# Spread of y about each partition's first channel, and an expert's transposes inside the next one's products

## The chip, the cores and the metric

The kernel runs on one core of one Trainium2 chip. The metric is the device time of one execution in microseconds, the median of three runs. One profiled execution of the same program gives the trace from which every other number here is taken.

## What is computed

The input x holds 4 sequences of 1024 tokens with 1024 channels. It is normalised over the channels (layernorm), and two branches are added to it:

```
xn  = layernorm(x)
out = x + attn(xn) + moe(xn)

attn:  q = xn @ Wq;  v = xn @ Wv                  # 16 heads of 64 channels
       state[t] = lam * state[t-1] + v[t]         # lam = sigmoid(beta), one for each head
       y  = q * state
       y  = (y - mean(y)) * rsqrt(var(y) + 1e-5) * ln_g + ln_b    # over the 1024 channels
       attn = (y * silu(xn @ Wg)) @ Wo

moe:   each of the 4096 tokens picks its best 8 of 64 experts (softmax of xn @ router.T);
       an expert takes at most the first 128 tokens that picked it
       h = silu(xg @ w1.T) * (xg @ v1.T);  yr = (h @ w2.T) * weight;  added back at the token's row
```

All data is fp32.

## The kernel before

**Attention part.** The four sequences (batches b = 0 to 3) are worked one after the other in `batch_row`. Channels lie on the 128 partitions, so a sequence's y is eight tiles of 128 partitions x 1024 tokens; y(c) is tile c, and a channel mean is a sum over the eight tiles and then over partitions. The tiles y(m) and y(m + 4) are made together in round m = 0 to 3: `states(m)` (v and the scan), then `queries(m)` (q times state). Four more rounds, `gates(m)`, follow.

Each round's matrix product is done with seven smaller products in place of eight (sums and differences of 512x512 blocks). `steps` writes them out. The blocks of xn are B11, B21, B22, B12 and their sums T1 to T4 (`right_sums`; T1 lies in B12's place); the results collect in three PSUM tags, a, b and c, of two banks each. The order on TensorE is B11 (bank a), B21 (b), then the last product of the round before, T1 (c), T2 (a), B22 (c), T3 (a), and T4 (a) only inside the next round. Between them ScalarE copies a bank (L148) and VectorE adds and reads the banks (L160, L169, L172).

In the records a fp32 product of 128x512 appears twice; `x8` in a profile line is four products.

**The statistics of y.** Variance is found from sums about a shift. After the first round (m = 0), `find_shift` takes sum1 = y(0) + y(4), has two products with the constant matrix mean_w spread the sum of all partitions (`all_channels`, tag r, one bank), and ScalarE copies it as `shift`. `less_shift` then subtracts the shift from each tile (VectorE, L621), squares it on ScalarE (L626), and GpSimd adds up squares and values (L627 sum2, L628 sum1). `find_spread` runs inside the product of `gates(0)`: two products for the mean, two for the mean square, VectorE subtracts (L661), ScalarE takes the root and VectorE the reciprocal (L663). `gates` then takes the mean from each tile (L677), scales by g and the reciprocal root (L678), adds b and multiplies by the gate (L681), and GpSimd's queue stores it to DRAM as `gated`.

In batch 0 the sums of the weight blocks (`left_sums`, L51 to L54) are made on GpSimd too, and tokens are chosen for the experts on VectorE meanwhile (`take`, the MAX8 and MATCH_REPLACE8 lines).

**Expert part.** `Experts.run` goes over the 64 experts. `hidden` makes two products of eight steps each (h in bank a and in bank b, 384 columns), ScalarE takes silu of the first (act), VectorE multiplies by the second. `output` turns act with three transposes on TensorE (hpt, L900), VectorE copies them out (hT, L901), six products give the expert's rows (y, L906), VectorE scales them (ys, L909), and GpSimd's queue adds them to `out` by an indirect DMA (L917). `fetch` loads the weights by SP's queue into the tiles that x and y had before, and gathers the tokens by GpSimd's queue (xg, L852) into the pool of nine blocks (`quarter`) that xn's blocks had; `turned` brings xg into the layout that TensorE wants (xgT, VectorE, L870). The products y @ Wo are spread as `project` over the experts, about a quarter of a unit for each. Wo's four blocks are loaded by `load_wo`, which also makes their sums T1 to T4 on VectorE (`right_sums`, four operations of 128x2048: L61, L64, L66, L68).

**What sets the order.** A scheduler orders each engine's instructions from the program text, and hands out the blocks of a pool in the order in which they come free. `in_order` pins the text's order for the engines that it is given; in the experts that is VectorE for the first three:

```
            kept = [mybir.EngineType.DVE] if e < 3 else []
            with in_order(self.tc, kept):
                act = self.hidden(e, self.turn)
                ...
                if before is not None:
                    self.output(*before)
```

Of the kernel before, what the change touches and what calls it, by code (L numbers as in the profile page):

```python
# [8 lines left out]
F32 = mybir.dt.float32  # L9
I32 = mybir.dt.int32  # L10
AF = mybir.ActivationFunctionType
ALU = mybir.AluOpType
# [4 lines left out]
P = 128  # L17
B, S, D = 4, 1024, 1024
NTOK = B * S
KD = D // P  # L20
# [77 lines left out]
class Pools:  # L98
# [21 lines left out]
    def y(self, name):  # L120
        return self.three.tile([P, 3, S], F32, tag="y", name=name)
# [111 lines left out]
def attn_and_routing(  # L233
# [345 lines left out]
    def batch_row(b, left):  # L579
# [5 lines left out]
        def y(c, cols=slice(0, S)):  # L585
            return ys[place[c] // 3][:, place[c] % 3, cols]

        shift = mean = ys[2][:, 2, :]
        sum1 = one.tile([P, S], F32, tag="sum1", name=f"sum1_{b}")
        sum2 = one.tile([P, S], F32, tag="sum2", name=f"sum2_{b}")  # L590
        spread = []
# [6 lines left out]
            )  # L598
            return ps

        def states(m, left, late):
# [9 lines left out]
            left = product(  # L611
                nc, pools, weights(b, 0, m), quarters[b],
                lo[:, H0], lo[:, H1], hi[:, H1], then, left, f"v_{b}_{m}", late,
                begun.get(0) if b == 0 and m == 0 else None,
            )
            return lo, hi, left

        def queries(m, lo, hi, left):
            def less_shift():
                for i, c in enumerate((m, m + KH)):  # L620
                    nc.vector.tensor_tensor(y(c), y(c), shift, ALU.subtract)  # L621
                    if m == 0 and i == 0:
                        nc.scalar.activation(sum2, y(c), AF.Square)
                        continue
                    sq = line.tile([P, S], F32, tag="line", name=f"sq_{b}_{c}")
                    nc.scalar.activation(sq, y(c), AF.Square)  # L626
                    nc.gpsimd.tensor_tensor(sum2, sum2, sq, ALU.add)  # L627
                    nc.gpsimd.tensor_tensor(sum1, y(0) if m == 0 else sum1, y(c), ALU.add)  # L628

            def find_shift():  # L630
                for h, cols in enumerate((H0, H1)):
                    ps = all_channels(sum1, h, f"sh_{b}_{h}")
                    nc.scalar.activation(shift[:, cols], ps, AF.Copy, scale=float(NM))
                less_shift()

            def then(c21):
                nc.vector.tensor_tensor(y(m + KH, H0), c21, hi[:, H0], ALU.mult)
                nc.vector.tensor_tensor(y(m), y(m), lo, ALU.mult)
                nc.vector.tensor_tensor(y(m + KH, H1), y(m + KH, H1), hi[:, H1], ALU.mult)
                if m == 0:  # L640
                    nc.gpsimd.tensor_tensor(sum1, y(0), y(KH), ALU.add)
                else:
                    less_shift()
# [6 lines left out]
            return left, find_shift if m == 0 else None  # L650

        def find_spread():

            for h, cols in enumerate((H0, H1)):
                ps = all_channels(sum1, h, f"mean_{b}_{h}")
                nc.scalar.copy(mean[:, cols], ps)
            rstd = one.tile([P, S], F32, tag="sum1", name=f"rstd_{b}")
            nc.scalar.activation(rstd, mean, AF.Square)
            for h, cols in enumerate((H0, H1)):
                ps = all_channels(sum2, h, f"var_{b}_{h}")  # L660
                nc.vector.tensor_tensor(rstd[:, cols], ps, rstd[:, cols], ALU.subtract)  # L661
            nc.scalar.activation(rstd, rstd, AF.Sqrt, bias=eps)
            nc.vector.reciprocal(rstd, rstd)  # L663
            spread.append(rstd)

        def gates(m, left):
            lo = line.tile([P, S], F32, tag="line", name=f"glo_{b}_{m}")
            hi = line.tile([P, S], F32, tag="line", name=f"ghi_{b}_{m}")

            def then(c21):  # L670
                (rstd,) = spread
                nc.scalar.activation(hi[:, H0], c21, AF.Silu)
                nc.scalar.activation(lo, lo, AF.Silu)
                nc.scalar.activation(hi[:, H1], hi[:, H1], AF.Silu)
                for i, (c, gate) in enumerate(((m, lo), (m + KH, hi))):
                    yc = y(c)
                    nc.vector.tensor_tensor(yc, yc, mean, ALU.subtract)  # L677
# [19 lines left out]
        late = None  # L697
        taking = take(b)
        for m in range(NM):
            lo, hi, left = states(m, left, late)  # L700
            if m == 0:
                route(b, logits[b])
            if b == 0 and m == 0:
# [8 lines left out]
            left, late = queries(m, lo, hi, left)  # L712
            next(taking)
            if b + 1 < B:
                if m == 1:
# [106 lines left out]
class Experts:  # L822
# [52 lines left out]
            self.tc.keep_in_program_order(done)  # L875
        return xT

    def hidden(self, e, xT):
        nc, pools = self.nc, self.pools
        ph = []  # L880
        for n in range(2):
            ps = pools.bank("ab"[n], [P, F], f"h{n}_{e}")
            w = self.weights.pop((e, n))
            for k in range(KD):
                nc.tensor.matmul(  # L885
                    ps, lhsT=xT[:, k, :], rhs=w[:, k, :], start=(k == 0), stop=(k == KD - 1)
                )
            ph.append(ps)
        act = pools.one.tile([P, F], F32, tag="cur", name=f"act_{e}")
        nc.scalar.activation(act, ph[0], AF.Silu)  # L890
        nc.vector.tensor_tensor(act, act, ph[1], ALU.mult)
        return act

    def output(self, e, act):
        nc, pools = self.nc, self.pools
        w2, wt = self.weights.pop((e, 2)), self.tokens.pop(e)[1]
        hT = pools.line.tile([P, KF, P], F32, tag="line", name=f"hT_{e}")
        pt = pools.bank("t", [P, KF, P], f"hpt_{e}")
        for j in range(KF):
            nc.tensor.transpose(pt[:, j, :], act[:, j * P : (j + 1) * P], self.ident)  # L900
        nc.vector.tensor_copy(hT, pt)  # L901
        ys = pools.line.tile([P, D], F32, tag="line", name=f"ys_{e}")
        for h, cols in enumerate((H0, H1)):
            ps = pools.bank("cr"[h], [P, SH], f"y_{e}_{h}")
# [21 lines left out]
    def load_wo(self):  # L926
        for name, (i, o) in zip(("B11", "B21", "B22", "B12"), BLOCKS):
            self.wo_b[name] = self.pools.block(f"wo_{name}")
            load_block(self.nc, self.wo_b[name], self.wo, i, o * SH, SH)
        right_sums(self.nc.vector, self.wo_b, lambda n: self.pools.block(f"wo_{n}"))  # L930

    def load_gated(self, u):
        t = self.pools.left.tile([P, NSLOT, KH, P], F32, tag="w", name=f"gated_{u}")
# [23 lines left out]
        self.turn = self.turned(0)  # L957

    def run(self):
        units = B * NM  # L960
        gated = self.load_gated(0)
        self.fetch(1)
        self.load_wo()
# [4 lines left out]
        before, todo, u, many = None, None, 0, iter(())  # L968
        for e in range(E):

            kept = [mybir.EngineType.DVE] if e < 3 else []
            with in_order(self.tc, kept):
                act = self.hidden(e, self.turn)
                self.fetch(e + 2)
                self.load(e + 1, 2)
                if e + 1 < E:
                    self.turn = self.turned(e + 1)
                if before is not None:
                    self.output(*before)
                before = e, act  # L980
                if u < units and e == begins[u]:
                    todo = self.project(u, gated)
# [54 lines left out]
```

## Time and profile before

| what | value |
|---|---|
| median of three runs | 2662.32 us (2661.1 to 2663.75) |
| the profiled execution | 2664.6 us, its span 2662.8 us |
| attention part | 0 to about 1237 us |
| expert part | about 1237 to 2662.8 us |
| TensorE busy | 2633.1 us, 6933 records |
| VectorE, ScalarE, GpSimd busy | 1086.5, 317.4, 732.9 us |
| mean granted TensorE clock | 0.997 |

The span is the time from the first to the last of the program's instructions. An engine's row of the timeline gives the start of a group, its length, the tile that it writes and those that it reads, and in square brackets the idle time of the engine just before it with what ended that. The stretch of half clock shows in the page's slices only as a share; the timeline shows it as groups that take twice their usual time.

### The profile page before, as it was taken

The page shows a single profiled execution, that of the slowest core. Times are in us where ns is not written, and L with a number is a line of the kernel's source. Part 1 is how long each engine was busy: PE and PEld are TensorE (multiplying, and loading weights), DVE is VectorE, ACT ScalarE, POOL GpSimd, SP SyncE. Part 2 cuts the span into 40 slices and gives each one's busy share as a digit, 9 for nine tenths or more (in the row PEclk, how much of TensorE's full clock was granted, in tenths as well). Part 3 has the DMA queues.
Part 4 walks back from the last instruction along what each step waited for, and adds up shares of the span by engine and source line. Part 5 has one row for each costly group of instructions (what it writes and reads, how often), then busy time and mean ns, then how long its engine had stood idle before and what let it go on. Part 6 is the DMA issues. An engine that isn't in the chain of part 4 may idle for free.

```text
span 2662.8 us, 18539 instructions
## 1 busy us (share of the span) xinstructions
PE 2633.1 (99%) x6933; PEld 1267.7 (48%) x6933; DVE 1086.5 (41%) x1394; ACT 317.4 (12%) x476; POOL 732.9 (28%) x655
## 2 busy tenths in 40 slices
PE   9999999999999999999999999999999999999997
PEld 5444444444444444444555555555555555555554
DVE  7945686465944685273222212222122221222211
ACT  4213112131212111121000000000000000000000
POOL 1453312121121102132333233332333333333321
PEclk9999999999999999999999999999999999999999
DMA  5665534452335522336889888898888988889886
GB/s 187 244 193 192 183 114 139 178 177 91 139 118 185 200 85 83 146 119 235 299 288 298 288 275 284 284 303 283 275 285 282 305 282 275 283 285 304 273 268 179
DMA packets 122473, 592.95 MB, mean 223 GB/s; under 512 B 15872, under 2 KB 52736, under 8 KB 89360
## 3 DMA queue, kind: packets, MB, share of 16 engines
q1 hardware_dynamic: 81488, 448.03, 46.4%
q0 software_dynamic: 40464, 143.72, 20.0%
q8 instruction: 55, 0.90, 0.1%
q14 instruction: 34, 0.28, 0.0%
q10 hardware_dynamic: 432, 0.01, 0.0%
HBM read 483.67 MB, written 124.81 MB: 229 GB/s over the span
## 4 chain that ended last, share of the span: by engine, by line
PE 94%; DVE 4%; issue 1%; DMA 0%; ACT 0%; POOL 0%; POOLq 0%; DVEq 0%
PE h L885 25%; PE y L906 13%; PE pa_o L137 8%; PE pa_g L137 8%; PE pa_q L137 7%; PE pa_v L137 7%; PE pc_o L137 4%; PE pc_v L137 4%; PE pc_g L137 4%; PE pc_q L137 4%; PE pb_o L137 2%; PE pb_g L137 2%; PE pb_q L137 2%; PE pb_v L137 2%; PE lg L475 1%; PE hpt L900 1%
## 5 line engine op out<-in xcount | busy, mean ns | idle before, releaser
L885 PE MATMUL h<-w,xgT 128*128 128x384 f32 x2048 | 672.2, 486 | 0.7 <-issue 0.7
L885 PEld LDWEIGHTS h<-w,xgT 128*128 128x128 f32 x2048 | 388.9, 190 | 286.2 <-issue 33.7
L852 POOL DMA_INDIRECT xg<-rows,tables x256 | 252.4, 986 | 679.8 <-DVE xgT L870 615.8
L906 PE MATMUL y<-w,hT 128*128 128x512 f32 x768 | 343.5, 597 | 1.6 <-DVE hT L901 1.6
L901 DVE COPY hT<-hpt 128x384 f32<-128x384 f32 x64 | 35.6, 556 | 729.1 <-PE hpt L900 729.1
L137 PE MATMUL pa_g<-xT,w 128*128 128x512 f32 x512 | 233.9, 600 | 2.7 <-DVE ghi L172 2.7
L906 PEld LDWEIGHTS y<-w,hT 128*128 128x128 f32 x768 | 140.9, 190 | 192.6 <-issue 153.3
L137 PE MATMUL pa_q<-xT,w 128*128 128x512 f32 x480 | 216.6, 593 | 3.8 <-DVE y L172 3.8
L137 PE MATMUL pa_v<-xT,w 128*128 128x512 f32 x480 | 216.5, 592 | 0.0
L909 DVE TENSOR_SCALAR ys<-y,wt 128x512 f32<-128x512 f32 x128 | 96.1, 751 | 202.2 <-PE y L906 199.7
L137 PE MATMUL pa_o<-wo_T,gated 128*128 128x512 f32 x384 | 177.8, 592 | 0.0
L137 PEld LDWEIGHTS pa_g<-xT,w 128*128 128x128 f32 x512 | 97.9, 192 | 127.1 <-issue 123.2
L137 PEld LDWEIGHTS pa_q<-xT,w 128*128 128x128 f32 x480 | 90.5, 190 | 116.8 <-issue 109.8
L137 PEld LDWEIGHTS pa_v<-xT,w 128*128 128x128 f32 x480 | 91.1, 190 | 114.9 <-issue 111.9
L890 ACT ACTIVATE act<-h 128x384 f32<-128x384 f32 x64 | 31.4, 490 | 848.6 <-PE hpt L900 833.3
L686 POOL DMA_DIRECT2D gated<-y x64 | 48.5, 763 | 301.3 <-DVE y L681 289.8
L917 POOL DMA_INDIRECT out_dram<-ys,tables x63 | 102.4, 1626 | 104.8 <-DMA out_dram<-ohi 76.1
L137 PE MATMUL pc_o<-wo_B,gated 128*128 128x512 f32 x256 | 117.1, 592 | 0.0
L137 PE MATMUL pc_g<-xT,w 128*128 128x512 f32 x256 | 115.2, 592 | 1.5 <-ACT sc_g L148 1.5
L137 PE MATMUL pc_v<-xT,w 128*128 128x512 f32 x256 | 115.3, 593 | 0.0
L137 PE MATMUL pc_q<-xT,w 128*128 128x512 f32 x256 | 115.2, 592 | 0.0
L628 POOL TENSOR_TENSOR sum<-sum,y 128x1024 f32<-128x1024 f32 x24 | 56.5, 2355 | 209.2 <-DVE y L621 209.2
(209 smaller groups left out, 2466.5 us busy)
## 6 DMA issues: line engine op xcount, KB each, us to landing
w<-in_w_dram SPq DMA_DIRECT2D x128, 1536.0 KB, 7.5
w<-in_v_dram SPq DMA_DIRECT2D x64, 1536.0 KB, 7.4
w<-wsum SPq DMA_DIRECT2D x36, 1792.0 KB, 8.1
wsum<-w POOLq DMA_DIRECT2D x12, 1792.0 KB, 6.5
x<-in_x_dram SPq DMA_DIRECT2D x32, 512.0 KB, 8.8
rows<-x POOLq DMA_DIRECT2D x32, 512.0 KB, 7.3
gated<-y POOLq DMA_DIRECT2D x64, 256.0 KB, 5.4
gated<-gated SPq DMA_DIRECT2D x16, 1024.0 KB, 8.1
```

What stands on the lines that cost most here:

```text
L137: nc.tensor.matmul(ps, lhsT=lhs[:, slot, k, :], rhs=blocks[right][:, k, :], start=start and k == 0, stop=stop and k == KH - 1, skip_group_ ...
L475: nc.tensor.matmul(two[h * E : (h + 1) * E, :], lhsT=r_sb[:, k, :], rhs=blocks[f"B{k // KH + 1}{h + 1}"][:, k % KH, :], start=(k == KD - 1 ...
L628: nc.gpsimd.tensor_tensor(sum1, y(0) if m == 0 else sum1, y(c), ALU.add)
L686: nc.gpsimd.dma_start(out=gated[b, :, :, slot, m, :].rearrange("u p j -> p u j"), in_=yc[:, h * SH : (h + 1) * SH].rearrange("p (u j) -> p ...
L852: nc.gpsimd.indirect_dma_start(out=xg[:, r, :], out_offset=None, in_=self.rows.rearrange("n (q c) -> (n q) c", q=NQ), in_offset=bass.Indir ...
L885: nc.tensor.matmul(ps, lhsT=xT[:, k, :], rhs=w[:, k, :], start=(k == 0), stop=(k == KD - 1))
L890: nc.scalar.activation(act, ph[0], AF.Silu)
L900: nc.tensor.transpose(pt[:, j, :], act[:, j * P : (j + 1) * P], self.ident)
L901: nc.vector.tensor_copy(hT, pt)
L906: nc.tensor.matmul(ps, lhsT=hT[:, j, :], rhs=w2[:, j, cols], start=(j == 0), stop=(j == KF - 1))
L909: nc.vector.tensor_scalar(ys[:, cols], ps, wt, None, ALU.mult)
L917: self.nc.gpsimd.indirect_dma_start(out=to, out_offset=bass.IndirectOffsetOnAxis(ap=rows, axis=0), in_=ys, in_offset=None, compute_op=ALU.add,
```

## The change

There are two parts.

In the statistics, the shift is no longer a mean that TensorE must find. Each tile's difference from y(0), the first channel of each partition, goes to a tile of its own (`away`), which ScalarE squares; y itself is not touched. `find_spread` corrects for the reference: with d = y(0) - mean, the sum of squares about the mean is sum2 + 2 d (sum1 - 8 y(0) + 4 d), worked out on VectorE in four operations (`off`). The sums of the last round (m = 3) go on VectorE, the others stay on GpSimd. The root is taken from the second product's bank by ScalarE directly, half by half.

In the experts, `turned_hidden` transposes the act of the expert before between the first and the second eight products of `hidden`, `output` follows with the six products, and the order on TensorE is pinned too for the first three experts. The sums of Wo leave `load_wo` and stand behind the gate of expert 0. The turn of the next expert's tokens stands behind the gate from expert 1 on.

```diff
-        shift = mean = ys[2][:, 2, :]
+        mean = ys[2][:, 2, :]
...
         def queries(m, lo, hi, left):
-            def less_shift():
-                for i, c in enumerate((m, m + KH)):
-                    nc.vector.tensor_tensor(y(c), y(c), shift, ALU.subtract)
-                    if m == 0 and i == 0:
-                        nc.scalar.activation(sum2, y(c), AF.Square)
-                        continue
-                    sq = line.tile([P, S], F32, tag="line", name=f"sq_{b}_{c}")
-                    nc.scalar.activation(sq, y(c), AF.Square)
-                    nc.gpsimd.tensor_tensor(sum2, sum2, sq, ALU.add)
-                    nc.gpsimd.tensor_tensor(sum1, y(0) if m == 0 else sum1, y(c), ALU.add)
-
-            def find_shift():
-                for h, cols in enumerate((H0, H1)):
-                    ps = all_channels(sum1, h, f"sh_{b}_{h}")
-                    nc.scalar.activation(shift[:, cols], ps, AF.Copy, scale=float(NM))
-                less_shift()
+            def collect(c):
+
+                add = (nc.vector if m == NM - 1 else nc.gpsimd).tensor_tensor
+                add(sum1, y(0) if c == KH else sum1, y(c), ALU.add)
+                away = line.tile([P, S], F32, tag="line", name=f"away_{b}_{c}")
+                nc.vector.tensor_tensor(away, y(c), y(0), ALU.subtract)
+                nc.scalar.activation(sum2 if c == KH else away, away, AF.Square)
+                if c != KH:
+                    add(sum2, sum2, away, ALU.add)
...
         def find_spread():
+            off = line.tile([P, S], F32, tag="line", name=f"off_{b}")
+            nc.vector.scalar_tensor_tensor(off, y(0), -float(KD), sum1, ALU.mult, ALU.add)
             for h, cols in enumerate((H0, H1)):
                 ps = all_channels(sum1, h, f"mean_{b}_{h}")
                 nc.scalar.copy(mean[:, cols], ps)
+            nc.vector.tensor_tensor(y(0), y(0), mean, ALU.subtract)
+            nc.vector.scalar_tensor_tensor(off, y(0), 0.5 * KD, off, ALU.mult, ALU.add)
+            nc.vector.tensor_tensor(off, off, y(0), ALU.mult)
+            nc.vector.scalar_tensor_tensor(sum2, off, 2.0, sum2, ALU.mult, ALU.add)
             rstd = one.tile([P, S], F32, tag="sum1", name=f"rstd_{b}")
-            nc.scalar.activation(rstd, mean, AF.Square)
             for h, cols in enumerate((H0, H1)):
                 ps = all_channels(sum2, h, f"var_{b}_{h}")
-                nc.vector.tensor_tensor(rstd[:, cols], ps, rstd[:, cols], ALU.subtract)
-            nc.scalar.activation(rstd, rstd, AF.Sqrt, bias=eps)
+                nc.scalar.activation(rstd[:, cols], ps, AF.Sqrt, bias=eps)
             nc.vector.reciprocal(rstd, rstd)
...
-    def hidden(self, e, xT):
+    def hidden(self, e, xT, before):
...
             ph.append(ps)
+            if n == 0 and before is not None:
+                hT = self.turned_hidden(*before)
+        return ph, hT
...
-        right_sums(self.nc.vector, self.wo_b, lambda n: self.pools.block(f"wo_{n}"))
...
-            kept = [mybir.EngineType.DVE] if e < 3 else []
+            kept = [mybir.EngineType.DVE, mybir.EngineType.PE] if e < 3 else []
             with in_order(self.tc, kept):
-                act = self.hidden(e, self.turn)
+                ph, turned_before = self.hidden(e, self.turn, before)
                 self.fetch(e + 2)
                 self.load(e + 1, 2)
-                if e + 1 < E:
+                if e == 0:
                     self.turn = self.turned(e + 1)
+                act = self.gate(e, ph)
+                if 0 < e < E - 1:
+                    self.turn = self.turned(e + 1)
+                if e == 0:
+                    right_sums(nc.vector, self.wo_b, lambda n: self.pools.block(f"wo_{n}"))
                 if before is not None:
-                    self.output(*before)
+                    self.output(*turned_before)
...
-        self.output(*before)
+        self.output(*self.turned_hidden(*before))
```

`turned_hidden` holds the transposes and the copy hT that stood in `output` before; `gate` holds the silu and the product that stood in `hidden`.

More of the change, by code (lines that the diff above doesn't have):

```diff
@@ L599, in all_channels, with states @@
             return ps
-        def states(m, left, late):
+        def states(m, left):
             lo = line.tile([P, S], F32, tag="line", name=f"lo_{b}_{m}")
@@ L612, in states @@
                 nc, pools, weights(b, 0, m), quarters[b],
-                lo[:, H0], lo[:, H1], hi[:, H1], then, left, f"v_{b}_{m}", late,
+                lo[:, H0], lo[:, H1], hi[:, H1], then, left, f"v_{b}_{m}", None,
                 begun.get(0) if b == 0 and m == 0 else None,
@@ L639, in then @@
                 nc.vector.tensor_tensor(y(m + KH, H1), y(m + KH, H1), hi[:, H1], ALU.mult)
[L640 to L643, printed above, removed]
+                for c in (m, m + KH):
+                    if c > 0:
+                        collect(c)
             left = product(
@@ L649, in queries @@
             )
-            return left, find_shift if m == 0 else None
+            return left
         def find_spread():
+            off = line.tile([P, S], F32, tag="line", name=f"off_{b}")
+            nc.vector.scalar_tensor_tensor(off, y(0), -float(KD), sum1, ALU.mult, ALU.add)
             for h, cols in enumerate((H0, H1)):
@@ L676, in then @@
                     yc = y(c)
-                    nc.vector.tensor_tensor(yc, yc, mean, ALU.subtract)
+                    if c > 0:
+                        nc.vector.tensor_tensor(yc, yc, mean, ALU.subtract)
                     nc.vector.scalar_tensor_tensor(
@@ L695, in gates @@
             )
-        late = None
         taking = take(b)
         for m in range(NM):
-            lo, hi, left = states(m, left, late)
+            lo, hi, left = states(m, left)
             if m == 0:
@@ L711, in batch_row @@
             next(taking)
-            left, late = queries(m, lo, hi, left)
+            left = queries(m, lo, hi, left)
             next(taking)
@@ L876, in turned @@
         return xT
-    def hidden(self, e, xT):
-        nc, pools = self.nc, self.pools
-        ph = []
+    def hidden(self, e, xT, before):
+        pools = self.pools
+        ph, hT = [], None
         for n in range(2):
@@ L884, in hidden @@
             for k in range(KD):
-                nc.tensor.matmul(
+                self.nc.tensor.matmul(
                     ps, lhsT=xT[:, k, :], rhs=w[:, k, :], start=(k == 0), stop=(k == KD - 1)
@@ L888, in hidden, with gate, turned_hidden @@
             ph.append(ps)
-        act = pools.one.tile([P, F], F32, tag="cur", name=f"act_{e}")
-        nc.scalar.activation(act, ph[0], AF.Silu)
-        nc.vector.tensor_tensor(act, act, ph[1], ALU.mult)
+            if n == 0 and before is not None:
+                hT = self.turned_hidden(*before)
+        return ph, hT
+    def gate(self, e, ph):
+        act = self.pools.one.tile([P, F], F32, tag="cur", name=f"act_{e}")
+        self.nc.scalar.activation(act, ph[0], AF.Silu)
+        self.nc.vector.tensor_tensor(act, act, ph[1], ALU.mult)
         return act
-    def output(self, e, act):
+    def turned_hidden(self, e, act):
         nc, pools = self.nc, self.pools
-        w2, wt = self.weights.pop((e, 2)), self.tokens.pop(e)[1]
         hT = pools.line.tile([P, KF, P], F32, tag="line", name=f"hT_{e}")
@@ L901, in output @@
         nc.vector.tensor_copy(hT, pt)
+        return e, hT
+    def output(self, e, hT):
+        nc, pools = self.nc, self.pools
+        w2, wt = self.weights.pop((e, 2)), self.tokens.pop(e)[1]
         ys = pools.line.tile([P, D], F32, tag="line", name=f"ys_{e}")
@@ L959, in run @@
     def run(self):
-        units = B * NM
+        nc, units = self.nc, B * NM
         gated = self.load_gated(0)
```

## The prediction

> **What bounds the kernel now.** I read the page first, then the groups of TensorE by line, and then, at each place where TensorE stops, the timeline of the engines around it.
>
> ```profile
> span 2662.8 us, 18539 instructions
> PE 2633.1 (99%) x6933; PEld 1267.7 (48%) x6933; DVE 1086.5 (41%) x1394; ACT 317.4 (12%) x476; POOL 732.9 (28%) x655
> ...
> PE 94%; DVE 4%; issue 1%; DMA 0%; ACT 0%; POOL 0%; POOLq 0%; DVEq 0%
> ```
>
> TensorE (PE) is busy 99% of the span and holds 94% of the chain of waits. So an edit pays in two ways only: it takes products off TensorE, or it removes one of its few stops. Work taken off VectorE (DVE, 41%), ScalarE (ACT, 12%) or GpSimd (POOL, 28%) is worth nothing by itself.
>
> A 512-column product appears as two records, started 0.429 us apart (pa_q x8 begins at 197.95, the next group at 201.39); a 384-column record takes 0.322 us (32 of h fill 1306.90 to 1317.22). From TensorE's timeline I listed each start that comes later than its predecessor's start plus this interval. Seven such places lie where the change touches the kernel. The largest:
>
> ```profile
> 1236.56 1.45 PE L885 MATMUL h<-w,xgT 128*128 128x384 f32 x4
> 1240.66 6.77 PE L137 MATMUL pa_g<-xT,w 128*128 128x512 f32 x8 [2.65 <-DVE ghi L172]
> 1247.27 9.19 PE L885 MATMUL h<-w,xgT 128*128 128x384 f32 x28
> ...
> 1234.91 2.29 DVE L61 TENSOR_TENSOR wo_T<-wo_B,wo_B 128x2048 f32<-128x2048 f32 x1 [9.98 <-DMA wo_B<-in_wo_dram]
> 1237.12 0.68 DVE L169 TENSOR_TENSOR glo<-pc_g,sc_g 128x512 f32<-128x512 f32 x1
> 1237.72 2.28 DVE L64 TENSOR_TENSOR wo_B<-wo_B,wo_B 128x2048 f32<-128x2048 f32 x1
> 1239.92 0.68 DVE L172 TENSOR_TENSOR ghi<-pa_g,sc_g 128x512 f32<-128x512 f32 x1
> ```
>
> The last product of the attention part waits for VectorE to read its bank (L172), and VectorE is busy with the sums of Wo (L61, L64). TensorE idles 2.65 us, and then eight records take 6.61 us (1240.66 to 1247.27) where 3.43 is usual.
>
> ```profile
> 132.62 0.70 PE L137 MATMUL pa_q<-xT,w 128*128 128x512 f32 x1 [1.82 <-DVE y L172]
> ...
> 240.80 3.67 PE L137 MATMUL pc_g<-xT,w 128*128 128x512 f32 x8 [1.48 <-ACT sc_g L148]
> 245.03 1.12 PE L596 MATMUL mean<-sum,mean_w 128*128 128x512 f32 x2 [0.56 <-POOL sum L628]
> ...
> 233.21 5.87 DVE L621 TENSOR_TENSOR y<-y 128x1024 f32<-128x1024 f32 x1
> ...
> 1257.18 0.55 PE L900 MATMUL hpt<-ident,act 128*128 128x128 f32 x3 [0.72 <-DVE act L891]
> 1258.38 0.88 PE L885 MATMUL h<-w,xgT 128*128 128x384 f32 x2 [0.65 <-issue]
> ...
> 2637.01 5.42 PE L906 MATMUL y<-w,hT 128*128 128x512 f32 x12 [0.65 <-DVE hT L901]
> ```
>
> At 132.6 (batch 0) VectorE's backlog is late with the read L172. At 240.8 ScalarE's copy sc_g stood behind a square that waited for a subtraction of 5.87 us, usually 1.2. At 1257 the transposes of expert 0 wait for its gate, and the next product waits for them; at 2637 the last but one expert waits for hT.
>
> [...] the 5.87 us subtraction ends 1.1 us after the GpSimd sum that ran 235.62 to 237.99. [...] Here 2.65 us were enough (the eight slow records); an idle stretch of 1.82 us (at 132.6) started none. [...]
>
> **The change part by part.** Orders of instructions are from the two built programs.
>
> *1. The product for the shift goes.* `find_shift` issues two products in each batch, 16 records in the trace (sh L596 x16). 16 x 0.429 = **6.9 us**, all on TensorE's path. No other product is added or removed.
>
> *2. Statistics.* Per batch, GpSimd loses six sums (15 to 9) of 2.35 us (L627, L628). VectorE loses eight subtractions of 1.2 us (L621), one of y's mean (L677) and two L661 of 0.68, 12.2 us; it gains seven `away` of 1.2, four sums of 1.2 in the last round, and in `find_spread` three scalar_tensor_tensor of 1.25 and two two-input ops of 1.2: 19.4 us. Plus 7 us a batch, hidden as long as TensorE's reads are not late. ScalarE loses two copies of 0.57, two squares of 1.06, and has two half square roots (estimate 0.7 each, from the 0.63 of a 128x512 silu) for one of 1.15; it gains two table loads of 1.28: about even. Nothing on SP's queue changes.
>
>  - Batch 0, 132.6: from 100 to 132 VectorE loses one subtraction net (1.2 us), and the two L290 groups that shared 105 to 111 with a GpSimd sum (4.89 and 3.57 us for two each, 1.5 when free). Walking its order with the free durations, L172 ends near 128.1; TensorE, 1.7 us earlier for the missing products, asks at 128.9. The **2.0 us** go, with under 1 us to spare.
>  - Batch 0, 240.8: the last sums are on VectorE, so nothing blocks the subtraction before the square. Of 1.64 + 0.72 us between starts I keep 0.2, for the first sum, which meets GpSimd's L52 to L54 at 229 to 233: **2.2 us** go.
>  - New wait: the products var need the corrected sum2. The program places the first one after three of the four products T4 of the first gate. Counted from the end of the gate's T3: TensorE gets there after mean (0.86), B11 and B21 (3.43 each) and T4 (2.57) = 10.3 us. VectorE starts 2.07 us after it (before: 249.42 to 251.49), then seven ops at spacings of 1.14 (L677) and 1.2 (L678), 8.15 us: 10.2 us. Level. From both sides: nothing, or up to 1 us each if one op is late; not below nothing. I take 0.15 x 4 = **0.6 us lost**. Behind it in VectorE's queue is the read glo of the next gate, which nothing needs for another 10 us.
>  - Two square roots with a table load each stand before ScalarE's copy of pc_g. By the same count, if the load waits for var as it did before, the copy ends 17.6 us after T3 and TensorE asks at 19.7. Cost nothing; 2 us of cover.
>
> *3. Sums of Wo behind expert 0's gate.* The four 2.29 us ops leave the reads of 1237 to 1240. The idle (2.82 us between starts) and the slow stretch go: 2.82 + 3.38 (with the two following starts) = **6.2 us**. Late next could be: hT of expert 0, behind three of the sums. Counted from the end of the last T4 (1247.27): act at 9.75, three sums to 16.6, hT to 17.2, asked for at 19.7. Next w2 of expert 0, whose tile is freed by gated writes. In the built program the gather of expert 2 now takes the block of T2 (free at 1229.7) and not that of T4, so GpSimd issues the four gathers before and not between those writes. The last is issued about 3.1 after T4 (it was 6.3), and w2 lands about 17.4 where it was 20.6; y asks at 19.7. Free by 2 us.
>
> *4. Transposes inside the next expert's products.* hpt of expert e follows the first eight products of e+1, by which time act is long ready; hT (0.56 us) hides under the second eight (5.15 us). At 1257 that frees 0.88 + 0.82 = **1.7 us**, at 2637 **0.8 us**; the end is a chain of scatters from y of expert 62, so this counts. In steady state TensorE has no stop there now (y starts are 22.72 us apart, worked out: 22.64), so 60 experts bring nothing.
>
> Sum: 6.9 + 2.0 + 2.2 - 0.6 + 6.2 + 1.7 + 0.8 = **19.2 us**. The profiled execution took 2664.6 us (its span and 1.8 around it), so it would take 2645.4. It lies 2.3 above the median of the three runs, 2662.3; from the median: **2643**.
>
> **The rivals.**
>  A. *Expert start stays late* (w2, hT or wo sums land after y asks). For: w2's margin is 2 us, of DMA times that vary by as much. Against: the free block. A stop of 1 to 2.7 us, with the slow stretch (3.4) if it is near 2.65: 2644 to 2649.
>  B. *The var products wait*, and the backlog at 132 stays. For: the count above is level, and lockouts by GpSimd doubled L681 to 2.29 us. Against: from batch 1 on GpSimd has no sums in that stretch. 1 to 2 us in each batch and the 2.0: 2649 to 2653.
>  C. *Slower*: hT at the experts' y. After the change y follows the second eight products directly, with no product of a projection between as filler. If VectorE's queue (ys, xgT, act ahead of hT) delays hT, TensorE stops once in each of 63 experts. The price is seen at 2637: 0.65 us idle. 63 x 0.65 = 41 us, less 19.2: 2684. It decides from 0.4 us an expert. Against: VectorE waits 729 us for hpt (L901), so it is idle when hT comes, and 5.15 us cover 0.56.
>  D. *Only the products' removal counts*, the stops being replaced by others of the same size: 2662.3 - 6.9 = 2655.
>
> **How the numbers follow.** Forecast 0.72 (own range 2640 to 2647), A 0.10, B 0.10, D 0.06, C 0.02. Below, the 58 gaps of 57 ns between y products (3.3 us in all) might close and no var wait come: 2639. Above, the range takes in A and the lower half of B: 2651. About 0.2% (5.3 us) is what a measurement of this kernel can tell from no change. Faster: forecast, A, B and half of D, 0.95; the same: the other half of D, 0.03; slower: C, 0.02.
>
> **What would show it.** Right: no sh group; 16 fewer records; TensorE without stops at 132, 240, 1237 and 1257; no stretch of half clock in mid span; hpt between two h groups, 63 times. Wrong: idle before var over 1 us; idle before y in each expert; L172 at 132 still late; y of expert 0 waiting for a DMA.

## The result and the profile after

The changed kernel takes 2642.89 us (median of four runs, 2641.28 to 2644.75), the kernel before beside it 2662.74. The ratio is 0.9926 with a 95% interval of 0.9909 to 0.9943: 19.9 us, or 0.74%, faster. Timed once more beside the experiments it took 2641.44 us against 2662.28 (0.9925, 0.9912 to 0.9939). The forecast was 2643, in a range of 2639 to 2651. So the number was right; several of its terms were not, and that their errors cancelled is luck.

The profiled execution took 2641.28 us, its span is 2639.3. The two traces differ by more than the medians, 23.5 us by span: the profiled execution of before lay 2.3 us above its median, that of the changed kernel 1.6 below. Of 46 executions of the kernel before that were timed beside the experiments, 20 show a mean clock of 0.997 (median 2663.1 us) and 26 show 0.998 (2660.9), and the profiled one, with its stretch of half clock (0.50 from 1240.05 to 1246.87 us), is of the first kind.

The top of the page, and the chain by engine:

```profile
span 2639.3 us, 18523 instructions
PE 2617.9 (99%) x6917; PEld 1269.6 (48%) x6917; DVE 1108.6 (42%) x1414; ACT 315.6 (12%) x472; POOL 696.5 (26%) x631
...
PE 95%; DVE 4%; issue 0%; DMA 0%; POOLq 0%; ACT 0%; DVEq 0%
```

TensorE has 16 records fewer, as worked out. VectorE works 22.1 us more and GpSimd 36.4 less (its 24 sums fewer would be 56 at 2.35 us each, but sums that were left ran longer, L622 at 3.3 us on average), and neither shows in the span as such: TensorE still holds nearly the whole chain.

Start of the experts, timeline of TensorE and of VectorE:

```profile
1226.48 3.60 PE L137 MATMUL pa_g<-xT,w 128*128 128x512 f32 x8
1229.92 14.36 PE L884 MATMUL h<-w,xgT 128*128 128x384 f32 x44
1244.11 0.49 PE L903 MATMUL hpt<-ident,act 128*128 128x128 f32 x3
1244.44 5.33 PE L884 MATMUL h<-w,xgT 128*128 128x384 f32 x16
1249.60 5.31 PE L914 MATMUL y<-w,hT 128*128 128x512 f32 x12
...
1239.69 2.28 DVE L61 TENSOR_TENSOR wo_T<-wo_B,wo_B 128x2048 f32<-128x2048 f32 x1
1242.01 2.29 DVE L64 TENSOR_TENSOR wo_B<-wo_B,wo_B 128x2048 f32<-128x2048 f32 x1
...
1246.55 0.55 DVE L904 COPY hT<-hpt 128x384 f32<-128x384 f32 x1
```

No line of TensorE has a wait in brackets, and every group has the length that its records make at full clock. Eight records of pa_g take 3.44 us to the next start (6.61 before). The sums of Wo now run under h. hT ends at 1247.1, 2.5 us ahead of y.

Batch 0, the read L172, timeline of GpSimd, VectorE and TensorE:

```profile
87.39 3.38 POOL L622 TENSOR_TENSOR sum<-y 128x1024 f32<-128x1024 f32 x1 [9.60 <-DVE y L630]
...
88.50 3.35 DVE L624 TENSOR_TENSOR away<-y 128x1024 f32<-128x1024 f32 x1
...
126.44 1.21 DVE L631 TENSOR_TENSOR y<-y,lo 128x1024 f32<-128x1024 f32 x1
127.69 1.22 DVE L624 TENSOR_TENSOR away<-y 128x1024 f32<-128x1024 f32 x1
128.83 0.68 DVE L172 TENSOR_TENSOR y<-pa_q,sc_q 128x512 f32<-128x512 f32 x1
...
129.57 3.70 PE L137 MATMUL pa_q<-xT,w 128*128 128x512 f32 x8 [1.02 <-DVE y L172]
```

This stop stayed, though shorter: the start at 129.57 is 1.18 us late (1.98 before, at 132.62). TensorE could have gone on at 128.4, so this is called the stop at 128 below. The read that it waits for (L172) stands behind a multiplication and a subtraction that TensorE does not wait for.

Batch 0, end of the statistics, timeline of TensorE, VectorE and ScalarE:

```profile
236.10 3.60 PE L137 MATMUL pc_g<-xT,w 128*128 128x512 f32 x8
239.54 1.02 PE L596 MATMUL mean<-sum,mean_w 128*128 128x512 f32 x2
...
254.13 1.10 PE L596 MATMUL var<-sum,mean_w 128*128 128x512 f32 x2
...
252.77 1.22 DVE L655 SCALAR_TENSOR_TENSOR sum<-off,sum 128x1024 f32<-128x1024 f32 x1
...
248.92 1.28 ACT L659 ACT_TABLE_LOAD   x1
...
255.27 0.69 ACT L659 ACTIVATE rstd<-var,eps 128x512 f32<-128x512 f32 x1 [5.06 <-PE var L596]
```

Both stops of before (at 240.8 and 245.0) are gone. The corrected sum2 ends at 253.99 and TensorE takes it at 254.13: level, as counted, and without a wait. The table load does not wait for var with its activation; it has been made 5 us ahead.

Two more changes stand in the trace that the prediction's sum does not have. The product kq in batch 3 was 0.84 us late before (the line is from the trace of before), and is on time now:

```profile
1138.80 0.46 PE L794 MATMUL kq<-ident,wide 64*128 64x64 f32 x4 [0.68 <-DVE wide L788]
```

And the loads of y's weights no longer wait. The group of these loads, first before, then after (the last columns are the idle time of the loader ahead of them, and what ended it):

```profile
L906 PEld LDWEIGHTS y<-w,hT 128*128 128x128 f32 x768 | 140.9, 190 | 192.6 <-issue 153.3 <-DVE hT L901 38.7
```

```profile
L914 PEld LDWEIGHTS y<-w,hT 128*128 128x128 f32 x768 | 145.9, 190 | 170.9 <-issue 153.0 <-DVE hT L904 1.2
```

Before, the loader waited 38.7 us in sum for hT, some 0.6 us an expert. Most of it lay under other products, but the load came so late that the second record of y started 57 ns late, in 58 experts: 3.3 us. Now hT is complete some 4 us before y, the loader runs ahead, and none of the 58 gaps is left.

### The profile page after: what moved, and what is told of

The parts are those of the page before. It is cut to its first block, busy times and chain, and to the rows that moved or that the text cites. A ratio compares the mean times of both kernels' runs of the same rounds, so it can differ in the third digit from the quotient of the medians.

```text
span 2639.3 us, 18523 instructions
## 1 busy us (share of the span) xinstructions
PE 2617.9 (99%) x6917; PEld 1269.6 (48%) x6917; DVE 1108.6 (42%) x1414; ACT 315.6 (12%) x472; POOL 696.5 (26%) x631
## 4 chain that ended last, share of the span: by engine, by line
PE 95%; DVE 4%; issue 0%; DMA 0%; POOLq 0%; ACT 0%; DVEq 0%
PE h L884 25%; PE y L914 12%; PE pa_g L137 8%; PE pa_o L137 8%; PE pa_q L137 7%; PE pa_v L137 7%; PE pc_g L137 4%; PE pc_o L137 4%; PE pc_v L137 4%; PE pc_q L137 4%; PE pb_o L137 2%; PE pb_g L137 2%; PE pb_q L137 2%; PE pb_v L137 2%; PE lg L475 1%; DVE cur L548 1%
## 5 line engine op out<-in xcount | busy, mean ns | idle before, releaser
L884 PE MATMUL h<-w,xgT 128*128 128x384 f32 x2048 | 682.1, 486 | 0.0
L856 POOL DMA_INDIRECT wt<-wtab,tables x64 | 62.3, 973 | 288.9 <-DVE ys L917 250.5
L895 DVE TENSOR_TENSOR act<-act,h 128x384 f32<-128x384 f32 x64 | 35.5, 554 | 229.6 <-PE h L884 229.6
L137 PEld LDWEIGHTS pa_o<-wo_T,gated 128*128 128x128 f32 x384 | 73.0, 190 | 90.9 <-issue 89.9
```

What stands on the lines that cost most here:

```text
L137: nc.tensor.matmul(ps, lhsT=lhs[:, slot, k, :], rhs=blocks[right][:, k, :], start=start and k == 0, stop=stop and k == KH - 1, skip_group_ ...
L856: nc.gpsimd.indirect_dma_start(out=wt, out_offset=None, in_=self.wtab, in_offset=bass.IndirectOffsetOnAxis(ap=self.idx[:, e : e + 1], axis=0),
L884: self.nc.tensor.matmul(ps, lhsT=xT[:, k, :], rhs=w[:, k, :], start=(k == 0), stop=(k == KD - 1))
L895: self.nc.vector.tensor_tensor(act, act, ph[1], ALU.mult)
```

## The experiments

Theory: TensorE's records and its stops set the time, each of them with its own cause, as the prediction summed them up. Rivals: only the removed products count; one half of the change brings all; stops are replaced by others. What the theory can't say before the runs: why the stops at 240 and before kq went, and whether the 57 ns gaps belong to the turn of act.

In what follows "late by" is from TensorE's timeline: a start compared with the start before it and the usual interval. The edits are shown in short.

**The two halves.** Expert half alone, statistics as before:

```
+ hidden(..., before): turned_hidden(*before) after the first eight products
+ right_sums(Wo) after the gate of expert 0        (statistics unchanged)
```

> The kernel before with the expert half of the change alone (hT turned inside the next expert's products, sums of Wo moved); the statistics stay as before. By stops on TensorE: the stop and slow stretch at the first expert (6.2), the stops at 1257 (1.7) and at the end (0.8) go, 8.7 us: about 2654.0 against 2662.7 before. If the 57 ns gaps between the y products of the steady state close as well (3.3): 12.0 us, about 2650.7. Rival, only the removal of the sh products counts: no gain here, about 2662.7. Rival, hT becomes late in each expert: slower than before.

Measured: 2652.16 us against 2661.76 (ratio 0.9965, 0.9952 to 0.9979), 9.6 us less. Its span is 12.4 us below that of before: the stops at 1237, 1257 and the last but one expert are gone, the slow stretch too, and so are all 58 gaps. The starts at 132.2, 240.4, 244.6 and 1138.4 are late as before (1.97, 1.64, 0.72, 0.84).

Statistics half alone, experts as before:

```
+ collect(c), find_spread() as changed             (Experts unchanged)
```

> The kernel before with the statistics half alone; the experts stay as before. By steps: 16 product records of 0.429 us (6.9), 0.8 of the stop at 132, 2.4 of the stops at 240 and 245, 0.84 of the stop before kq in batch 3: 10.9 us, about 2651.8. Rival, only the products' removal counts: 6.9, about 2655.8. Rival, waits for var give something back: 2653 to 2655. If the two halves are independent, this gain and that of the expert half add up to that of the whole change (19.9).

Measured: 2651.74 us against 2661.76 (0.9967, 0.9955 to 0.9979), 10.0 us less; the rival of 6.9 alone falls. The two gains make 19.6, the whole change 19.9 and 20.8 in its two timings: within their intervals, some 3.5 us each way, the halves add up. But the trace (span 2648.2) is 14.6 below before, 3.7 more than the step sum. Its start of the experts, timeline of TensorE:

```profile
1225.17 1.45 PE L882 MATMUL h<-w,xgT 128*128 128x384 f32 x4
1229.21 3.70 PE L137 MATMUL pa_g<-xT,w 128*128 128x512 f32 x8 [2.60 <-DVE ghi L172]
1232.75 9.19 PE L882 MATMUL h<-w,xgT 128*128 128x384 f32 x28
```

The stop is the same as before, 2.60 us of idle (2.65 there), yet the eight records behind it run at full clock (3.54 us to the next start, 6.61 before). So the slow stretch of 3.4 us that the prediction put into the sum is not a fixed consequence of that stop. Over all traces, past the first 30 us, starts that were late by 2.5 us or more were followed by slow records of 1.6 to 3.4 us in seven of nine places (the first expert in `before`, `before_without_y3_sums` and `wo_sums_early`, the second in `turn_before_y`, and batch 0 in `last_sums_gpsimd`, `wo_sums_early` and `before_without_y3_sums`); late starts of 2.2 us or less (2.20 in `turn_before_y`, 1.98 in before) never were.

The two places without are this one and the first y of the run `turn_before_y` below, which was late by 2.93 us. In the trace of before the granted clock stood at 0.50 from 1240.05 to 1246.87, 6.82 us, which costs 3.4. What tells the seven places from the two is not shown. So this stop cost 6.2 us in the trace of before, with the slow stretch, and 2.75 here by its late start, without.

That such stretches make the two kinds of executions of before is argued from the mean clock (3.4 us in 2662 are 0.0013), not seen: only one of them is traced, and a stretch half as long would be lost in the rounding.

**The products by themselves.**

```
+ def idle_products(): all_channels(y(0), h, ...) for both h     # nobody reads the result
  product(..., f"v_{b}_{m}", idle_products if m == 1 else None, ...)
```

> The changed kernel with two products of y(0) with mean_w a batch put back where the sh products were; nothing reads their result and nothing waits for it. By TensorE time: 16 records of 0.429 us, 6.9 us more than the changed kernel, about 2649.8; gain against before about 13. Rival, the products filled stops of TensorE and cost nothing: about 2643. Rival, what cost time was the wait of the row behind them, not they: well under 6.9.

The group of the added products in the trace:

```profile
L596 PE MATMUL sh<-y,mean_w 128*128 128x512 f32 x16 | 8.2, 593 | 0.0
```

Measured: 2647.15 us. That is 4.3 more than the changed kernel's first median (2642.89) and 5.7 more than its second (2641.44), and 6.9 by span (2646.2 against 2639.3). They cost time on TensorE though nothing waits for them. The 6.9 is partly by chance: next to them, in batches 0 and 3, two starts are late by 0.66 and 0.96, and in return the stop at 128 vanished (1.18), because TensorE came there later and VectorE's backlog was done. That fits a stop made by VectorE being behind, not by a fixed wait.

**The last sums on GpSimd again.**

```
- add = (nc.vector if m == NM - 1 else nc.gpsimd).tensor_tensor
+ add = nc.gpsimd.tensor_tensor
```

> The changed kernel with the sums of m = 3 on GpSimd again, as those of m < 3 are. If GpSimd's sums lock VectorE and so made the stops at 240 (L160 late) and before kq in batch 3: kq stop of 0.8 us back, part or all of 2.4 us at 240 back; 0.8 to 3.2 us more, 2643.7 to 2646; VectorE rows beside a GpSimd sum take 1.5 us or more where they took 0.2 to 1.2. The var products stay in time, since sum2 is complete some 14 us before the row that asks for it. Rival, the stops went because ScalarE and find_shift left the path: no change, about 2643. Rival, GpSimd's sums end after the mean and var products ask: a wait in each batch, over 4 us more.

Measured: 2650.51 us (0.9959, 0.9945 to 0.9972), 7.6 to 9.1 us more than the changed kernel in its two timings, well over the 0.8 to 3.2 expected. VectorE and GpSimd in batch 0, and TensorE in batches 0 and 3:

```profile
230.22 8.17 DVE L624 TENSOR_TENSOR away<-y,y 128x1024 f32<-128x1024 f32 x1
...
229.76 2.35 POOL L622 TENSOR_TENSOR sum<-sum,y 128x1024 f32<-128x1024 f32 x1
...
232.63 2.37 POOL L627 TENSOR_TENSOR sum<-sum,away 128x1024 f32<-128x1024 f32 x1
234.95 2.35 POOL L622 TENSOR_TENSOR sum<-sum,y 128x1024 f32<-128x1024 f32 x1
...
240.10 6.25 PE L137 MATMUL pc_g<-xT,w 128*128 128x512 f32 x8 [3.78 <-ACT sc_g L148]
...
1154.17 1.13 PE L596 MATMUL mean<-sum,mean_w 128*128 128x512 f32 x2 [1.23 <-POOL sum L622]
```

A subtraction of 1.2 us takes 8.17: it lasts through three GpSimd sums, and ends 1.1 us after the third. Behind it ScalarE's square and its copy sc_g are late, and with them pc_g by 3.94 us, with 2.65 us of slow records. In batch 3 GpSimd's last sums stand behind eight gathers, and the mean products are late by 1.39 and 1.16; that part is GpSimd's own lateness and not VectorE held up beside a GpSimd sum. All these together make the 9.1 us between the spans. So the lock of the expectation, which is that hold-up, cost 3.94 us here and the slow records behind it, more than I put it at. One part of the expectation failed: kq was on time. The sum of y 3 on GpSimd starts as soon as the multiplication L631 is done (1130.12) and ends at 1132.47, just after the first integer row has begun (1132.32, 0.20 us). In the kernel before it followed a further subtraction of y, and fell on those rows. Hence the next run.

**The hold-up, shown on the kernel before.** In each of batches 0 and 3 two GpSimd sums are left out, so the variance there lacks tile 3; no other engine's order changes:

```
+ if b in (0, B - 1) and c == NM - 1:
+     continue
  nc.gpsimd.tensor_tensor(sum2, sum2, sq, ALU.add)
  nc.gpsimd.tensor_tensor(sum1, ..., y(c), ALU.add)
```

> The kernel before, leaving out of sum1 and sum2 the two GpSimd sums of channel group 3 (y 3 and its square) in batches 0 and 3; every other engine keeps its order. If GpSimd's sums lock VectorE: L621 at 233 takes about 1.2 us instead of 5.87, the stop of TensorE at 240 (1.5) and that before the mean products (0.6 to 0.7) go, and the integer row before kq takes 0.2 us instead of 1.46, so that the stop at 1138 (0.84) goes: 2.9 to 3.2 us less than before, about 2659. Rival, these rows were late for another reason (squares on ScalarE, the wait for find_shift): they keep their length and the stops stay, about 2662.

VectorE's timeline of this run:

```profile
235.63 1.22 DVE L621 TENSOR_TENSOR y<-y 128x1024 f32<-128x1024 f32 x1
...
1135.97 0.18 DVE L761 TENSOR_SCALAR int_s<-int_s 128x64 int32<-128x64 int32 x1
1136.07 0.18 DVE L764 TENSOR_SCALAR int_s<-int_s 128x64 int32<-128x64 int32 x1
```

The integer row and the sum beside it in the kernel before:

```profile
1136.11 1.46 DVE L759 TENSOR_SCALAR int_s<-int_s 128x64 int32<-128x64 int32 x1
...
1135.17 2.35 POOL L628 TENSOR_TENSOR sum<-sum,y 128x1024 f32<-128x1024 f32 x1 [31.01 <-DVE y L621]
```

Measured: 2658.25 us against 2662.28 (0.9988, 0.9981 to 0.9994), 4.0 less; 3.2 were expected from 1.64 + 0.72 + 0.84. L621 takes 1.22 in place of 5.87, the integer row 0.18 in place of 1.46 (that one ended with the sum, at 1137.5), and all three stops are gone. This is a cause shown: with these sums out of the way both stops near 240 and that before kq disappear. How much of the one at 245 is the hold-up stays open: there TensorE waited for GpSimd's own last sum, and two sums fewer bring that forward too. In this traced execution the stop at 132, which the edit does not aim at, was longer (3.03 us, with 1.75 of slow records, against 1.98) and the slow stretch at the first expert shorter, so its span is only 2.7 below; the medians, over 21 and 25 executions, are the better measure. How a sum comes to hold up a row of VectorE is not shown: the integer row ended with its one sum, and the subtraction of 8.17 us in the run before lasted through three.

**The sums of Wo back in load_wo.**

```
- if e == 0: right_sums(nc.vector, self.wo_b, ...)      # in run, behind the gate
+ right_sums(self.nc.vector, self.wo_b, ...)            # end of load_wo
```

> The changed kernel with the four sums of Wo back in load_wo, ahead of the experts; everything else as changed. By the stop on TensorE: the transpose of the first expert's rows waits for sums on VectorE again, a stop of about 2.8 us before the T4 products or the next h, and in the executions where the granted clock drops behind it 3.4 us more: 2.8 to 6.2 us over the changed kernel, 2645.7 to 2649.1, with single times in two groups some 3 us apart, the later at the lower mean clock. Rival, the turn of act inside the next products had removed that stop by itself: about 2643. Rival, sums on the path of the first y wherever they stand: about 2643.

Timeline of TensorE and of VectorE:

```profile
1234.25 5.30 PE L137 MATMUL pa_g<-xT,w 128*128 128x512 f32 x8 [3.90 <-DVE ghi L172]
...
1228.50 2.29 DVE L61 TENSOR_TENSOR wo_T<-wo_B,wo_B 128x2048 f32<-128x2048 f32 x1 [11.21 <-DMA wo_B<-in_wo_dram]
1230.71 0.69 DVE L169 TENSOR_TENSOR glo<-pc_g,sc_g 128x512 f32<-128x512 f32 x1
1231.31 2.28 DVE L64 TENSOR_TENSOR wo_B<-wo_B,wo_B 128x2048 f32<-128x2048 f32 x1
1233.51 0.69 DVE L172 TENSOR_TENSOR ghi<-pa_g,sc_g 128x512 f32<-128x512 f32 x1
```

Measured: median 2645.1 us, the five times in two groups: 2644.1, 2644.2, 2645.1 at a mean clock of 0.998, and 2650.5, 2650.9 at 0.997. The stop is back, and L61 waits for the DMA of wo_B there (11.21 us of idle time ahead of it); that the size of the stop goes with that DMA is my estimate from this order. In the traced execution (2650.85) it is 4.06 us with 1.71 of slow records; the other 3.8 us of that execution's excess lie at 93 to 135 in batch 0, where the stop at 128 was 2.71 with 1.77 of slow records. So the step is right in its mechanism, and worth 2.7 us (the earlier group against 2641.44) to 5.8 (this trace), not always 6.2. The groups are 6 apart rather than the 3 that I expected; in the one execution of the later group that is traced, two places had slow records.

**The turn of act back in front of y.**

```
- if n == 0 and before is not None: hT = self.turned_hidden(*before)    # in hidden
- self.output(*turned_before)
+ self.output(*self.turned_hidden(*turned_before))      # hidden now hands `before` back as it is
```

> The changed kernel with act turned directly ahead of its own y products again, as before; sums of Wo and statistics as changed. If this turn makes the 57 ns gaps between the y products (58, 3.3 us) and the stops at the first y (up to 1.7) and at the last but one (0.8): 3.3 to 5.8 us more than the changed kernel, 2646.2 to 2648.7. Rival, the gaps came from elsewhere: 0.8 to 2.5 us more and 58 gaps absent. Rival, the turn is hidden either way: about 2643.

VectorE and TensorE at the first y, and the group of y's weight loads:

```profile
1247.71 2.29 DVE L68 TENSOR_TENSOR wo_T<-wo_B,wo_T 128x2048 f32<-128x2048 f32 x1
1251.37 0.55 DVE L893 TENSOR_TENSOR act<-act,h 128x384 f32<-128x384 f32 x1 [1.37 <-ACT act L892]
1251.84 1.24 DVE L867 STREAM_TRANSPOSE xgT<-xg 128x1024 f32<-128x1024 f32 x1
1253.00 0.52 DVE L902 COPY hT<-hpt 128x384 f32<-128x384 f32 x1
...
1253.58 5.42 PE L912 MATMUL y<-w,hT 128*128 128x512 f32 x12 [2.77 <-DVE hT L902]
```

```profile
L912 PEld LDWEIGHTS y<-w,hT 128*128 128x128 f32 x768 | 141.5, 190 | 195.9 <-issue 154.8 <-DVE hT L902 40.3
```

Measured: 2654.39 us, 11.5 above the changed kernel, twice what I expected. The 58 gaps are back (3.3), and the loader's wait for hT too (40.3). But the first experts now lose more than the old 1.7. At the first, act and xgT of the next expert stand before hT in the pinned order of VectorE, behind the sums of Wo, and y is late by 2.93. At the second, the next h is late by 2.54, with 1.6 of slow records behind it; it starts 0.1 us after xgT is complete. With 0.81 at the last but one and 1.0 more at 128 (2.20; a scan at 116.2 took 2.28 us, and 1.26 in the changed kernel) this makes 12.2 of the 12.4 us between the spans. The early turn and the moved sums belong together: behind expert 0's gate the sums are harmless only as long as hT is made early.

**A version that beats both.** Two orders pinned in the changed kernel:

```
+ low = nc.vector.tensor_tensor(y(m), y(m), lo, ALU.mult).ins
+ if b == 0: keep low behind c22 on VectorE
+ pools.pin = keep_in_program_order if m == 0 and 0 < b < B - 1    # T4 of q 3 behind pb_g 0
```

> The changed kernel with two orders pinned: in batch 0 the multiplication y(m) by lo stays behind the sum c22 on VectorE, so that c22 of q 0 comes about 2.4 us earlier and T4 at 128 doesn't wait (1.18 us); in batches 1 and 2 the T4 products of q 3 stay behind the first eight products of g 0, so that c22 has time there (2 stops of 1.17 us). 3.5 us less than the changed kernel, 2639.4, TensorE without stops at 128, 519 and 822. Rival, other rows of VectorE become late by the moved ones (var products of batches 1 and 2 wait, c21 comes 7 us later there): 0 to 2 us less or a loss.

Measured: 2637.69 us against 2662.01 (0.9907, 0.9892 to 0.9922). VectorE and TensorE at the two places:

```profile
127.12 0.68 DVE L175 TENSOR_TENSOR y<-pa_q,sc_q 128x512 f32<-128x512 f32 x1
127.72 1.21 DVE L634 TENSOR_TENSOR y<-y,lo 128x1024 f32<-128x1024 f32 x1
...
128.75 3.60 PE L138 MATMUL pa_q<-xT,w 128*128 128x512 f32 x8
...
519.15 3.60 PE L138 MATMUL pa_g<-xT,w 128*128 128x512 f32 x8
522.58 3.60 PE L138 MATMUL pb_g<-xT,w 128*128 128x512 f32 x8
526.01 3.60 PE L138 MATMUL pa_q<-xT,w 128*128 128x512 f32 x8
```

No wait at 128, and in batches 1 and 2 sixteen records now lie between the products that L175 reads and the T4 products. To settle its size, it and the changed kernel were timed on one chip:

> The changed kernel itself, timed on the same chip as the next one: 2643 by its earlier median, in one group of times, since it has no stop over 1.3 us.

> The two pinned orders again, beside the changed kernel: the traces differ by 3.5 us (three stops of 1.17), so 3.5 us less than after_beside if the times follow the stops; 5 us or more if the changed kernel's stop at 128 is often longer than in its trace.

Measured: 2641.44 and 2637.77 us, 3.7 apart, against 3.5 from three stops of 1.17. Their ratios to before have overlapping intervals (0.9912 to 0.9939 and 0.9894 to 0.9925), but the five times of the one (2641.07 to 2642.97) and the four of the other (2637.65 to 2638.03) don't overlap.

## Why the prediction was right, and where it wasn't

| step | predicted | in the traces |
|---|---|---|
| 1. products for the shift | 6.9 | 6.9 |
| 2. stop at 132 | 2.0 | 0.8 |
| 2. stops at 240 and 245 | 2.2 | 2.4 |
| 2. wait for var | -0.6 | 0 |
| 3. sums of Wo: stop, slow stretch | 2.8 + 3.4 | 2.8 + 3.4 |
| 4. stops at 1257 and at the end | 1.7 + 0.8 | 1.7 + 0.8 |
| kq in batch 3 | not seen | 0.8 |
| y's weights, 58 gaps | 0, named as the low end | 3.3 |
| sum | 19.2 | 22.9 |

The span differs by 23.5; of the rest 0.4 is an earlier start of the first transposes, which the change doesn't touch.

Late starts under 0.3 us, other than the 58 gaps, are not counted.

*Step 1* is right and separately shown: two idle products bring 6.9 us back in the trace, in part by chance, and 4.3 to 5.7 in the medians.

*Step 2, the stop at 132,* is the mis-sized term: 0.8 of 2.0. I walked VectorE's order from 100 with free durations and kept the state that before had there. But the change had already put a subtraction at 88.5, next to the first GpSimd sum, where it took 3.35 us, and VectorE's read that was at 96.72 before came at 98.84. L172 ended at 129.5 in place of 128.1, and TensorE came at 128.4 in place of 128.9. "Under 1 us to spare" was really 1.2 us short. No run moves that subtraction alone, so that it is the reason is read from the trace. Rival B named this backlog, and was right in that half. Pinning the read ahead of two rows removed the stop. The prediction's reading of the L290 rows has a slip besides: the two groups share a row, and the three rows took 5.62 us together, 3.3 more than when free. Its 128.1 fits with these 3.3 (132.6 less 3.3 and 1.2), so the slip did no harm.

*Step 2, the stops at 240,* is right in cause and nearly in size: without GpSimd's sums of group 3 they are gone.

*Step 2, var:* the count was level and came out level (253.99 against 254.13); of the 0.6 only two starts, 0.08 us late each, came. The table load, put down as waiting for var, ran ahead, so its cover was larger than I wrote.

*Step 3* is right for the traced execution. Against the median it was overstated, because the 3.4 us of slow clock were counted as if every execution had them. The kernel with the statistics half alone has the stop (2.60 us of idle, 2.65 before) without them; why is not shown.

*Step 4* is right where it saw a stop. Its sentence that 60 experts bring nothing was wrong: it read TensorE's starts, found 22.72 against 22.64 us and passed over the 0.08, and kept the 58 gaps only as its low end. The line that tells what they are was at hand, the weight loads of y waiting 38.7 us for hT.

*kq* was missed because I listed the stops at the places that the change touches in the text. A hold-up of VectorE beside a GpSimd sum has no place in the text: the sum that made this stop was GpSimd's, the row that it hit belonged to the choice of tokens.

Against the median these errors cancel: 3.3 and 0.8 gained unseen, 0.6 not lost, 1.2 lacking, and the slow stretch not in every execution. Before's executions at clock 0.998 (2660.9) are 19.5 above the changed kernel's 2641.4, and the traces' 22.9 less 3.4 is 19.5 as well; that fits, but since none of them is traced it does not show that they had no slow stretch. Rivals A, C and D are out: no DMA or hT is late at the experts, and more than the products counts.

## What to carry to other kernels

When one engine is busy 99% of the time, list all its late starts and look for what made each, also away from the edited lines; and read the waits of its weight loads as well as of its products, since a load that came just in time cost 57 ns in each of 58 rounds here. Before a slow row of VectorE is blamed on its place in the queue, look at what GpSimd runs beside it: a subtraction of 1.2 us lasted 8.17 here, through a series of three GpSimd sums. And before a difference is taken from one trace, ask whether the stretch at lower clock in it belongs to every execution: the same stop can cost its own length, or that and 3.4 us more.

## What the runs showed of the hardware

- A VectorE subtraction of 128x1024, 1.21 us at 1136.34 in `last_sums_gpsimd` with no GpSimd sum beside it, took 8.17 us at 230.22 in the same trace, where three GpSimd sums of 2.35 to 2.37 us lay beside it with gaps of 0.52 us or less; it ended 1.1 us after the third.
- An integer tensor_scalar of 128x64 took 1.46 us in the trace of before, beside a GpSimd sum, and 0.18 us in `before_without_y3_sums`, where that sum is left out. Three rows that read PSUM during the same sum (L172, L758 and L774 in before) took 0.69, 0.21 and 0.27 us in both traces.
- After a stop of 2.65 us TensorE's granted clock stood at 0.50 for 6.82 us in the trace of before. After one of 2.60 at the same place of the program, in `statistics_only`, eight records took 3.54 us to the next start, against 6.61 in before. What decides it is not shown.
- A table load was made at 248.92 to 250.20 us in the trace of after, 5 us ahead of the activation that it was for (255.27), while that activation waited 5.06 us for its input.
